# An attention block followed by eight experts: the first expert's loads put into the last batch, powers two experts ahead, gate rows apart, last output through six PSUM banks

## The chip, the cores and the metric

The kernel runs on one core of one Trainium2 chip. The metric is device time in microseconds of one execution; the time before is the median of three runs. The profile is of one further execution. Engines are called as the profile calls them: PE (TensorE, matmuls; PEld is its weight load), DVE (VectorE), ACT (ScalarE), POOL (GpSimd) and SP (SyncE, which here only issues transfers).

## What is computed

The block takes x of 16 batches x 1024 rows x 256 columns, all in float32. From a condition vector per batch come six modulation vectors (shift, scale and gate for each of two halves; a gate keeps its sign and a size of at least 0.25).

- First half: h = layernorm(x) * (1 + scale) + shift. Then an attention layer on h: another layernorm with gamma and beta, q, k and v projections with biases, rotary positions, 16 heads of 16 columns, causal softmax, output projection, and h added again. x = x + gate * that.
- Second half: h = layernorm(x) * (1 + scale) + shift with the second set of vectors, read as one list of 16384 rows. Eight experts each take 512 rows of h (their row numbers are given; a row may be drawn by several experts and more than once by one), compute gelu(rows W1 + b1) W2 + b2 (256 to 1024 to 256 columns), times a combine weight, and add the result to the rows. Only the first 2048 of the combine weights' rows exist; larger row numbers take the last one. x = x + gate * the sum.

## The kernel before, in words

The kernel has a start, an attention stage and an experts stage. On PE, DVE, ACT and POOL the order of the instructions is the order of the program, written out by hand (`manual_schedule`). SP is not in that list: its transfers are placed by the framework's scheduler, by when they become ready in its own model, and the queue is then fixed. So a transfer that waits holds those behind it in SP's queue.

**Start.** The modulation vectors are computed (lines 112 to 143) and written to two tables in device memory, `mod_a` for the first half and `mod_b` for the second, 3 x 256 columns each. Weights and rotary tables are loaded and turned (165 to 216). Two buffers in device memory, `ops`, in which the operands of the score products are laid out per head as 32 rows, get their fixed rows filled by 64 small transfers (line 259). Then the first batch's x is loaded and prepared.

**Attention.** Batches are worked one after another. A batch has four groups of four heads, a group twelve blocks: `(c, j)`, c the half of the 1024 queries (512 each), j the block of 128 keys, causal ones only. Per block and head, `product` in `attend` (line 513) makes the scores in a tile of the PSUM pool `ps_s` (six banks, tag `s`), ACT makes the exponential (526), POOL masks the diagonal blocks (528), and `values` (549) multiplies with v one block later. In the same block the *next* group's row maxima are found (`maxima`: PE 455, DVE 467 and 471), in banks of the same pool. `place` sends them through device memory into the operands (491, 492). All other work of a batch hangs in the list `extra`, at a block number: preparation of the next batch, the layernorms of the one after, and the output projection of the batch before (`project`: `turn` at 591 transposes, ACT copies at 592, `out_` at 598 multiplies with Wo, DVE 608 multiplies with the gate, POOL 611 adds x for two row blocks at once, and SP 612 writes them to `out`). `wide` and `narrow` are lists of block numbers in a batch; `t` and `w` are these for the batch at hand. The projection's `pn` and `pw` tiles are in pool `ps_1`, tag `misc`, with one bank. x of a batch stays in SBUF from its load to its output; four buffers (`bufs=4`, line 269) rotate.

The last batch has no next batch, so its last group has no maxima beside it. Its own output projection has nothing to hide behind: half 0 is turned at the last two blocks, and the rest follows after the last block:

```
        behind[0](*blocks[-1])
        behind[1](1)()
        for items in [proj[B - 1][0][1], *proj[B - 1][1]]:
            for item in items:
                item()
```

**Experts.** Their pools (`fc`, `fw`, `fk`, `fps`) open when the attention's have closed, in the same memory. Each expert e has these steps:

- `weights(e)`: SP loads W1, W2 and b2, two buffers each.
- `rows_mod(e)`: POOL gathers, per 128 rows, the second half's modulation rows (768 columns, four gathers). `rows_x(e)`: four gathers of x's rows from `out`. A gather is one POOL instruction (line 102).
- `hidden(e)`: statistics on DVE (818, 821), the power -0.5 on POOL (823, 824), normalizing on DVE (827), scale and shift (830, 831).
- `turned(e)`: eight transposes on PE (840), DVE copies (841). `first(e)`: 32 matmuls (849), ACT's gelu (852), which starts with a table load.
- `often(e)`: how often each row occurs in the expert's list, on DVE (859 to 861), from `tokb`, a copy of all lists in every partition (four transfers of 512 KB, line 892).
- `rows_now(e)`: four gathers of the rows of `out` as they are now (`cur`).
- `second(e)`: 64 matmuls (874) in four products of 128 rows; DVE adds b2 (877), multiplies with count, weight and gate (878), adds `cur` (881); POOL scatters the 128 rows to `out` (883). PSUM holds two such products.

All rows of x for all experts must have been gathered before the first scatter. The order of the stage is the end of the program: `weights(0)`, `weights(1)`, `rows_mod(0)`, `rows_x(0)`, `often(0)`, `hidden(0)`, `turned(0)`, `rows_mod(1)`, `rows_x(1)` to `rows_x(7)`, and then for each expert `hidden(e + 1)`, `first(e)`, `often(e + 1)`, `turned(e + 1)`, `rows_now(e)`, `second(e)`, `weights(e + 2)`, `rows_mod(e + 2)`.

Of the kernel before, what the change touches and what calls it, by code (L numbers as in the profile page):

```python
# [19 lines left out]
P = 128  # L20
# [7 lines left out]
def adaln_block_kernel(  # L28
# [81 lines left out]
    mod_b = dram.tile([B, 3 * D], F32, name="mod_b")  # L110


    with tc.tile_pool(name="mod", bufs=1) as mp, tc.tile_pool(
# [17 lines left out]
        for half, dst in ((0, mod_a), (1, mod_b)):  # L131
# [11 lines left out]
            nc.sync.dma_start(out=dst[:, :], in_=m3)  # L143
# [14 lines left out]
    )  # L158
    with ExitStack() as actx:
# [107 lines left out]
        def load(b):  # L267
            s = S[b]
            s["x"] = two.tile([P, NT, D], F32, name=f"x_{b}", tag="x", bufs=4)
# [311 lines left out]
        def project(b):  # L581
# [4 lines left out]
            def turn(c, k):  # L586
                if k == 0:
                    oTs[c] = wk.tile([P, KC, QC], F32, name=f"onT_{b}_{c}", tag="onT")
                pt = ps_1.tile([P, TC, P], F32, name=f"pn_{b}_{c}_{k}", tag="misc")
# [4 lines left out]
            def out_(c, t):  # L594
                t0 = c * TC + t
                po = ps_1.tile([P, D], F32, name=f"pw_{b}_{t0}", tag="misc")
# [12 lines left out]
                if t % 2 == 0:  # L609
                    return  # L610
# [77 lines left out]
        for b in range(B):  # L688
# [19 lines left out]
            if b > 0:  # L708
# [8 lines left out]
            if b + 1 == B:  # L717
                pn, pw = proj[b][0]
                each(pn, [at0 + NG * NS - 2, at0 + NG * NS - 1])
# [12 lines left out]
        for b in range(B):  # L732
            for G in range(NG):
# [3 lines left out]
                for n, (c, j) in enumerate(blocks):  # L737
# [29 lines left out]
                    if n == NS - 2 or n == 2 and behind:  # L767
                        turn()
# [5 lines left out]
        for items in [proj[B - 1][0][1], *proj[B - 1][1]]:  # L774
            for item in items:
                item()


    FF = W1.shape[2]
    NF = FF // P  # L780

# [6 lines left out]
    X = [dict() for _ in range(E)]  # L788
# [3 lines left out]
    times = fc.tile([P, E, NCT], F32, name="times")  # L792

    def weights(e):
        s = X[e]
        s["w1"] = fw.tile([P, KC, FF], F32, name=f"w1_{e}", tag="w1")
        nc.sync.dma_start(out=s["w1"], in_=W1[e].rearrange("(k p) f -> p k f", p=P))
        s["w2"] = fw.tile([P, NF, D], F32, name=f"w2_{e}", tag="w2")
        nc.sync.dma_start(out=s["w2"], in_=W2[e].rearrange("(k p) d -> p k d", p=P))
        s["b2"] = fw.tile([P, D], F32, name=f"b2_{e}", tag="b2")  # L800
        nc.sync.dma_start(out=s["b2"], in_=b2[e].partition_broadcast(P))

    def rows_mod(e):
        X[e]["mod"] = fw.tile([P, NCT, 3 * D], F32, name=f"modg_{e}", tag="modg")
        for t in range(NCT):
            gather(X[e]["mod"][:, t, :], mod_b[:, :], bidx[:, t, e : e + 1])

# [3 lines left out]

    def hidden(e):

        s = X[e]
        xe = xg[:, e, :, :]
        st = fk.tile([P, NCT, 6], F32, name=f"fst_{e}", tag="fst")
        for t in range(NCT):
            nc.vector.bn_stats(st[:, t, :], xe[:, t, :])
        mv = fk.tile([P, NCT, 2], F32, name=f"fmv_{e}", tag="fmv")
        for t in range(NCT):  # L820
            nc.vector.bn_aggr(mv[:, t, :], st[:, t, :])
        rstd = fk.tile([P, NCT], F32, name=f"frstd_{e}", tag="frstd")
        nc.gpsimd.tensor_tensor(rstd, mv[:, :, 1], eps[:, :NCT], ALU.add)
        nc.gpsimd.tensor_tensor(rstd, rstd, mhalf[:, :NCT], ALU.pow)
        hn = fk.tile([P, NCT, D], F32, name=f"hn_{e}", tag="hn")
        for t in range(NCT):
            nc.vector.tensor_scalar(
                hn[:, t, :], xe[:, t, :], mv[:, t, 0:1], rstd[:, t : t + 1], ALU.subtract, ALU.mult
            )
# [38 lines left out]
    def second(e):  # L868
        s = X[e]
        y = fk.tile([P, NCT, D], F32, name=f"fy_{e}", tag="fy")  # L870
        for t in range(NCT):
            po = fps.tile([P, D], F32, name=f"fo_{e}_{t}", tag="fo")
            for f in range(NF):
# [5 lines left out]
                y[:, t, :], y[:, t, :], times[:, e, t : t + 1], s["mod"][:, t, 2 * D : 3 * D], ALU.mult, ALU.mult  # L879
# [16 lines left out]
    weights(0)  # L896
    weights(1)
    rows_mod(0)
    rows_x(0)
    often(0)  # L900
    hidden(0)
    turned(0)
    rows_mod(1)

    for e in range(1, E):
        rows_x(e)
    for e in range(E):
# [3 lines left out]
        if e + 1 < E:  # L911
            often(e + 1)
            turned(e + 1)
        rows_now(e)
        second(e)
# [72 lines left out]
```

## Time and profile before

| what | value |
|---|---|
| time, median of 3 runs | 3397.24 us (3396.8 to 3398.42) |
| time of the profiled execution | 3397.8 us |
| its span, first to last instruction | 3396.1 us |
| mean granted clock of PE | 0.953 |
| busy: PE, DVE, ACT, POOL | 3138.8, 2308.1, 1727.4, 1216.3 us |
| last matmul of values in the attention (line 549) starts | 3065.77 us |
| last output rows issued (line 612) | 3089.72 us |
| first matmul of the first expert (line 849) | 3116.99 us |
| first matmul of the second expert (line 849) | 3174.99 us |

The page cuts the span into 40 equal slices of 85 us. A digit is the busy share of an engine in that slice, in tenths; the row PEclk is the clock that PE was granted, in tenths of full speed:

```profile
PE   1589999999999999999999999999999999994888
DVE  1267777877777777777777777777777777652544
ACT  0135656565555565555555565656565655551111
POOL 1334243333434343334343434333342443114443
PEclk6579999999999999999999999999999999997899
DMA  6101011121111111111111111212111111004442
```

The attention fills slices 3 to 36, the experts the last four.

### The profile page before, as it was taken

Reading aid. Unit: us, or ns where it says so; the run is one execution under the profiler, and the core shown is the slowest. Engines: PE = TensorE matmul, PEld = TensorE weight load, DVE = VectorE, ACT = ScalarE, POOL = GpSimd, SP = SyncE. Lnnn points to the kernel's source line nnn. Section 1 sums busy time; section 2 is a strip of 40 time slices with the busy share of each in tenths; the row PEclk is TensorE's granted clock in tenths of the full one; section 3 lists DMA queues with packets and bytes.
Section 4 is the critical chain, followed back from the end, with each engine's and each line's share of the span. In section 5 each row is a group of like instructions: output and inputs, shape, how many; then the busy total and the mean of one; then the engine's idle time right before and its main releaser. Section 6 shows DMA issues by size and latency. Waiting matters only on the chain.

```text
span 3396.1 us, 62141 instructions
## 1 busy us (share of the span) xinstructions
PE 3138.8 (92%) x22497; PEld 1371.5 (40%) x22497; DVE 2308.1 (68%) x6919; ACT 1727.4 (51%) x3916; POOL 1216.3 (36%) x1338
## 2 busy tenths in 40 slices
PE   1589999999999999999999999999999999994888
PEld 0244344434344444444444444344434444332556
DVE  1267777877777777777777777777777777652544
ACT  0135656565555565555555565656565655551111
POOL 1334243333434343334343434333342443114443
PEclk6579999999999999999999999999999999997899
DMA  6101011121111111111111111212111111004442
GB/s 149 48 19 51 27 45 62 39 68 38 57 45 46 55 48 58 46 56 48 47 51 50 54 53 42 65 39 68 33 62 40 49 43 46 33 11 165 148 148 88
DMA packets 105827, 199.10 MB, mean 59 GB/s; under 512 B 14704, under 2 KB 60176, under 8 KB 105520
## 3 DMA queue, kind: packets, MB, share of 16 engines
q1 hardware_dynamic: 97328, 169.83, 16.2%
q0 software_dynamic: 8192, 25.31, 2.3%
q8 instruction: 177, 2.90, 0.4%
q14 instruction: 130, 1.06, 0.1%
HBM read 135.21 MB, written 59.88 MB: 57 GB/s over the span
## 4 chain that ended last, share of the span: by engine, by line
PE 80%; POOL 4%; ACT 4%; DVE 3%; issue 3%; DMA 1%; POOLq 0%; DVEq 0%; ACTq 0%
PE s L513 35%; PE o L549 17%; PE pqk L370 8%; PE m L455 5%; PE pv L397 4%; PE pw L598 4%; PE fo L874 3%; ACT p L526 3%; POOL p L528 2%; PE pn L591 1%; PE ptx L354 1%; ACT h L307 1%; DMA modg<-mod_b,bidx 1%; DVE mt L467 1%; PE pm L487 1%
## 5 line engine op out<-in xcount | busy, mean ns | idle before, releaser
L526 ACT ACTIVATE p<-s 128x512 f32<-128x512 f32 (+3 forms) x3072 | 1336.1, 489 | 1066.5 <-PE m L455 970.1
L455 PE MATMUL m<-ko,qo 32*128 32x512 f32 (+3 forms) x6144 | 1590.0, 541 | 10.4 <-DVE mt L471 7.0
L513 PE MATMUL s<-qo,ko 32*128 32x512 f32 (+3 forms) x6144 | 1486.3, 537 | 2.7 <-ACT p L526 0.4
L467 DVE TENSOR_REDUCE mt<-m 128x1 f32<-128x512 f32 x1024 | 658.3, 685 | 233.0 <-PE m L455 204.7
L513 PEld LDWEIGHTS s<-qo,ko 32*128 32x128 f32 x6144 | 513.2, 184 | 666.2 <-issue 474.1
L528 POOL TENSOR_SCALAR_AFFINE_SELECT p<-p 128x512 f32<-128x512 f32 x512 | 325.9, 637 | 1055.6 <-ACT p L526 1054.6
L471 DVE CUSTOM_DVE_ANT_0 masked<-m,dmask,mt 128x512 f32<-128x512 f32 (+3 forms) x1024 | 562.3, 549 | 203.8 <-PE m L455 101.1
L549 PE MATMUL o<-p,v_pad 128*32 128x512 f32 (+3 forms) x6144 | 656.0, 499 | 47.4 <-POOL p L528 44.5
L471 DVE CUSTOM_DVE_ANT_0 masked<-m,dmask 128x512 f32<-128x512 f32 (+3 forms) x1024 | 501.2, 489 | 265.8 <-PE m L455 177.3
L455 PEld LDWEIGHTS m<-ko,qo 32*128 32x128 f32 x6144 | 574.5, 185 | 64.0 <-DVE mt L471 25.5
L370 PE MATMUL pqk<-xnT,wqk 128*128 128x256 f32 x1024 | 307.8, 425 | 15.4 <-DVE rot L376 13.7
L549 PEld LDWEIGHTS o<-p,v_pad 128*32 128x32 f32 x6144 | 121.2, 108 | 487.9 <-POOL p L528 260.6
L370 PEld LDWEIGHTS pqk<-xnT,wqk 128*128 128x128 f32 x1024 | 183.6, 200 | 215.3 <-issue 119.9
L389 POOL TENSOR_TENSOR rot<-rot,rot 128x512 f32<-128x512 f32 x64 | 81.6, 1275 | 374.1 <-DVE rot L376 290.3
L611 POOL TENSOR_TENSOR y<-y,x 128x512 f32<-128x512 f32 x64 | 81.8, 1279 | 303.2 <-DVE y L608 265.2
L471 DVE DVE_READ_ACCUMULATOR2_ANT mt<- 128x1 f32 x2048 | 169.7, 83 | 0.2
L320 POOL TENSOR_TENSOR h<-h,mod 128x512 f32<-128x512 f32 x128 | 162.6, 1274 | 5.6 <-ACT h L307 4.2
L376 DVE SCALAR_TENSOR_TENSOR rot<-pqk,bcol,cosT 128x256 f32<-128x256 f32 x256 | 122.9, 480 | 57.1 <-PE pqk L370 46.4
L598 PE MATMUL pw<-wo_sb,onT 128*128 128x256 f32 x512 | 148.5, 413 | 4.9 <-DVE y L608 3.3
L852 ACT ACTIVATE gT<-ph,b_sb 128x512 f32<-128x512 f32 x64 | 43.9, 687 | 209.9 <-PE ph L849 190.6
L397 PE MATMUL pv<-wv_sb,xnT 128*128 128x256 f32 x512 | 147.4, 411 | 3.3 <-ACT v_pad L404 2.3
L598 PEld LDWEIGHTS pw<-wo_sb,onT 128*128 128x128 f32 x512 | 88.7, 193 | 106.5 <-issue 47.5
(105 smaller groups left out, 2346.7 us busy)
## 6 DMA issues: line engine op xcount, KB each, us to landing
ops<-rot SPq DMA_DIRECT2D x128, 256.0 KB
qo<-ops SPq DMA_DIRECT2D x64, 512.0 KB
ko<-ops SPq DMA_DIRECT2D x64, 512.0 KB
x<-in_x_dram SPq DMA_DIRECT2D x16, 1024.0 KB
out_dram<-y SPq DMA_DIRECT2D x64, 256.0 KB
w<-in_W_dram SPq DMA_DIRECT2D x16, 1024.0 KB
mod<-mod_a SPq DMA_DIRECT2D x16, 384.0 KB
ops<-zeros SPq DMA_DIRECT2D x62, 64.0 KB
```

The source lines that it names most:

```text
L320: nc.gpsimd.tensor_tensor(h, h, row(n), op)
L370: nc.tensor.matmul(ps, lhsT=wqk[:, k, n, e, :], rhs=xt[:, k, ts(u, QW)], start=(k == 0), stop=(k == KC - 1))
L376: nc.vector.scalar_tensor_tensor(s["rot", e, f][:, ts(u, QW)], ps, bcol[:, n, e : e + 1], tab[:, half * QC + u * QW : half * QC + (u + 1) ...
L397: nc.tensor.matmul(pv, lhsT=S[b]["xnT", t // TC][:, k, ts(t % TC, P)], rhs=wv_sb[:, k, :], start=(k == 0), stop=(k == KC - 1),)
L455: nc.tensor.matmul(sc[:, 0:w], lhsT=q[rows, ts(i, P)], rhs=k[rows, c * QC : c * QC + w], start=True, stop=True,)
L467: nc.vector.tensor_reduce(dst, sc[:, 0:w], AX.X, ALU.max, negate=True)
L471: nc.vector.tensor_tensor_reduce(out=masked[:, 0:w], in0=sc[:, 0:w], in1=dmask[:, QC - w : QC], scale=-1.0, scalar=mt[half][:, 0, h, i % T ...
L513: nc.tensor.matmul(sc[:, 0:w], lhsT=k[rows, ts(j, P)], rhs=q[rows, q0 : q0 + w], start=True, stop=True,)
L526: nc.scalar.activation(p[:, h, 0:w], sc[:, 0:w], AF.Exp, scale=scale)
L528: nc.gpsimd.affine_select(out=p[:, :, 0:P], in_=p[:, :, 0:P], compare_op=ALU.is_ge, fill=0.0, base=0, pattern=[[0, GH], [1, P]], channel_m ...
L549: nc.tensor.matmul(acc[c][W * g : W * (g + 1), QC - w : QC], lhsT=v[:, j, h * VW : h * VW + W], rhs=ps[c, j][:, g, 0:w], start=(j == 0), s ...
L598: nc.tensor.matmul(po, lhsT=oTs[c][:, k, ts(t, P)], rhs=wo_sb[:, k, :], start=(k == 0), stop=(k == KC - 1),)
```

## The change

In the text of the program:

- A pool `big` with four buffers of 8 KB per partition is opened before the attention's pools and stays to the end. x of the batches, W1 and W2 of all experts and the first expert's modulation rows take its buffers in turn. W1, the modulation rows and W2 of the first expert are placed in the last batch: W1 and the tile at block 2, the four gathers at blocks 4 to 7 of group 1, W2 at block 8 of group 2.
- `mod_b` loses the gate columns; they get a table `mod_g` and gathers of their own (`rows_gate`).
- In the last batch the projection of the batch before moves to earlier blocks. Half 0 of the last batch's own projection is done within its last group (turned at blocks 7 and 8, multiplied at 8 to 11), after `turn` of half 0 at block 6 instead of 10. The tiles `pn` and `pw` of the last batch are taken from the six banks of `ps_s`. For half 1 DVE adds x and each 128 rows are written by themselves.
- In the experts `hidden` is split: `stats(e)` on DVE, `powers(e)` on POOL, and the rest. Statistics and powers of expert e + 2 and its modulation rows come within expert e, ahead of `second(e)`. Before the loop the gathers of x for experts 1 and 2 come first, then the second expert's powers, then the first expert's gate rows, then the x rows of experts 3 to 7. `often(0)` stays ahead of the first statistics.

The diff, cut to its core:

```
     mod_a = dram.tile([B, 3 * D], F32, name="mod_a")
-    mod_b = dram.tile([B, 3 * D], F32, name="mod_b")
+    mod_b = dram.tile([B, 2 * D], F32, name="mod_b")
+    mod_g = dram.tile([B, D], F32, name="mod_g")
...
-            nc.sync.dma_start(out=dst[:, :], in_=m3)
+            if half == 0:
+                nc.sync.dma_start(out=mod_a[:, :], in_=m3)
+            else:
+                nc.sync.dma_start(out=mod_b[:, :], in_=m3[:, 0 : 2 * D])
+                nc.sync.dma_start(out=mod_g[:, :], in_=g)
...
+    big = ctx.enter_context(tc.tile_pool(name="big", bufs=4))
...
+    def big_tile(shape, name):
+        return big.tile(shape, F32, name=name, tag="x")
+
+    def weights_1(e):
+        X[e]["w1"] = big_tile([P, KC, FF], f"w1_{e}")
+        nc.sync.dma_start(out=X[e]["w1"], in_=W1[e].rearrange("(k p) f -> p k f", p=P))
+
+    def weights_2(e):
+        X[e]["w2"] = big_tile([P, NF, D], f"w2_{e}")
+        nc.sync.dma_start(out=X[e]["w2"], in_=W2[e].rearrange("(k p) d -> p k d", p=P))
+
+    def first_mod():
+        X[0]["mod"] = big_tile([P, NCT, 2 * D], "modg_0")
+
+    def rows_mod(e, t):
+        gather(X[e]["mod"][:, t, :], mod_b[:, :], bidx[:, t, e : e + 1])
...
-            s["x"] = two.tile([P, NT, D], F32, name=f"x_{b}", tag="x", bufs=4)
+            s["x"] = big_tile([P, NT, D], f"x_{b}")
...
-                pt = ps_1.tile([P, TC, P], F32, name=f"pn_{b}_{c}_{k}", tag="misc")
+                if b + 1 == B:
+                    pt = ps_s.tile([P, QC], F32, name=f"pn_{b}_{c}_{k}", tag="s").rearrange("p (t q) -> p t q", q=P)
+                else:
+                    pt = ps_1.tile([P, TC, P], F32, name=f"pn_{b}_{c}_{k}", tag="misc")
...
-                po = ps_1.tile([P, D], F32, name=f"pw_{b}_{t0}", tag="misc")
+                if b + 1 == B:
+                    po = ps_s.tile([P, QC], F32, name=f"pw_{b}_{t0}", tag="s")[:, :D]
+                else:
+                    po = ps_1.tile([P, D], F32, name=f"pw_{b}_{t0}", tag="misc")
...
-                if t % 2 == 0:
+                if (b, c) == (B - 1, NC - 1):
+                    nc.vector.tensor_tensor(y[:, t % 2, :], y[:, t % 2, :], s["x"][:, t0, :], ALU.add)
+                    nc.sync.dma_start(
+                        out=out[b * L + t0 * P : b * L + (t0 + 1) * P, :], in_=y[:, t % 2, :]
+                    )
+                if t % 2 == 0 or (b, c) == (B - 1, NC - 1):
                     return
...
-            if b > 0:
+            if b + 1 == B:
+                for c, (pn, pw) in enumerate(proj[b - 1]):
+                    each(pn, t[2 * c : 2 * c + 2])
+                    each(pw, w[8 * c + 8 : 8 * c + 12])
+                at(2, [lambda: weights_1(0), first_mod])
+                at(2 * NS + 8, [lambda: weights_2(0)])
+                for n in range(NCT):
+                    at(NS + TC + n, [lambda n=n: rows_mod(0, n)])
+                end = at0 + 3 * NS + mid + 3
+                pn, pw = proj[b][0]
+                each(pn, [end, end + 1])
+                each(pw, range(end + 1, end + 5))
+            elif b > 0:
                 for c, (pn, pw) in enumerate(proj[b - 1]):
                     each(pn, t[3 + 2 * c : 5 + 2 * c])
                     each(pw, (w[18:22], w[26:30])[c])
...
-            if b + 1 == B:
-                pn, pw = proj[b][0]
-                each(pn, [at0 + NG * NS - 2, at0 + NG * NS - 1])
...
-                    if n == NS - 2 or n == 2 and behind:
+                    if n == (NS - 2 if units else mid + 2) or n == 2 and behind:
                         turn()
...
-        for items in [proj[B - 1][0][1], *proj[B - 1][1]]:
+        for items in proj[B - 1][1]:
...
+    def stats(e):
         st = fk.tile([P, NCT, 6], F32, name=f"fst_{e}", tag="fst")
         for t in range(NCT):
-            nc.vector.bn_stats(st[:, t, :], xe[:, t, :])
+            nc.vector.bn_stats(st[:, t, :], xg[:, e, t, :])
         for t in range(NCT):
-            nc.vector.bn_aggr(mv[:, t, :], st[:, t, :])
+            nc.vector.bn_aggr(mv[:, e, t, :], st[:, t, :])
+
+    def powers(e):
+        nc.gpsimd.tensor_tensor(rstd[:, e, :], mv[:, e, :, 1], eps[:, :NCT], ALU.add)
+        nc.gpsimd.tensor_tensor(rstd[:, e, :], rstd[:, e, :], mhalf[:, :NCT], ALU.pow)
...
-    weights(0)
-    weights(1)
-    rows_mod(0)
+    bias_2(0)
...
     rows_x(0)
     often(0)
+    stats(0)
+    powers(0)
     hidden(0)
     turned(0)
-    rows_mod(1)
-
-    for e in range(1, E):
+    later_mod(1)
+    rows_x(1)
+    rows_x(2)
+    stats(1)
+    powers(1)
+    rows_gate(0)
+
+    for e in range(3, E):
         rows_x(e)
+    weights_1(1)
+    weights_2(1)
+    bias_2(1)
     for e in range(E):
         if e + 1 < E:
             hidden(e + 1)
...
             often(e + 1)
             turned(e + 1)
+        if e + 2 < E:
+            stats(e + 2)
         rows_now(e)
+        if e + 1 < E:
+            rows_gate(e + 1)
+        if e + 2 < E:
+            powers(e + 2)
+            later_mod(e + 2)
         second(e)
         if e + 2 < E:
-            weights(e + 2)
-            rows_mod(e + 2)
+            weights_1(e + 2)
+            weights_2(e + 2)
+            bias_2(e + 2)
```

`later_mod(e)` is four `rows_mod(e, t)` into a tile of its own pool, `rows_gate(e)` four gathers from `mod_g`.

## The prediction

> **What bounds the kernel now.** I read the page's 40 slices first: TensorE is at 90% or more from the fourth slice to the 36th, then falls to 4 and 8, its clock row falls to 7, and the DMA row, at 0 to 2 since the second slice, rises to 4. So the attention is bound by TensorE, and what can be won lies in the last 350 us. I then read the chain of waits between attention and experts.
>
> ```profile
> 3068.54 1.11 PE pw L598 x4
> ...
> 3077.87 2.09 PE pw L598 x4
> ...
> 3084.46 3.96 issue
> 3088.46 1.24 POOL y L611
> 3089.72 3.34 DMA out_dram<-y
> 3093.12 0.72 issue
> 3093.84 0.96 POOL modg L102
> ...
> 3102.70 6.12 DMA xg<-out_dram,idx
> ...
> 3124.47 28.93 issue
> 3153.40 0.07 DVE hn L827
> ```
>
> The columns are start, length, what. Eight output projections go one by one through a single PSUM bank, then the last rows are written, then four gathers of modulation rows stand ahead of the four of x. The 28.93 us are no idle engine. The timeline of GpSimd shows what runs in them:
>
> ```profile
> 3123.55 0.94 POOL L102 DMA_INDIRECT xg<-out_dram,idx  x1 [0.30 <-issue]
> ...
> 3151.06 0.95 POOL L102 DMA_INDIRECT xg<-out_dram,idx  x1 [0.30 <-issue]
> 3152.03 0.21 POOL L823 TENSOR_TENSOR frstd<-fmv,eps 128x4 f32<-128x4 f32 x1
> 3152.32 1.05 POOL L824 TENSOR_TENSOR frstd<-frstd,mhalf 128x4 f32<-128x4 f32 x1
> ```
>
> The second expert's power is queued behind 28 gathers, one per 1.255 us. TensorE waits 24.85 us for it (its transposes at 3157.47). In the experts stage, the same timeline:
>
> ```profile
> 3254.83 1.00 POOL L883 DMA_INDIRECT out_dram<-fy,idx  x1 [6.62 <-DVE fy L881]
> 3260.96 0.99 POOL L883 DMA_INDIRECT out_dram<-fy,idx  x1 [5.12 <-DVE fy L881]
> 3264.18 0.97 POOL L883 DMA_INDIRECT out_dram<-fy,idx  x1 [2.23 <-DVE fst L818]
> 3270.59 0.97 POOL L883 DMA_INDIRECT out_dram<-fy,idx  x1 [5.44 <-issue]
> ```
>
> Each scatter writes `out` and waits until the one before has landed: 3.2 us is the usual spacing (2.41 to land and 0.77, as the chain's last scatter shows), 6.1 and 6.4 are two slow landings. Behind them stood the modulation rows and the power that the next expert needed, so this expert took 39.1 us (chain: fo at 3248.59, then 3287.72), the others 29.1 to 30.8.
>
> **Start of the kernel.** x moves into a pool that opens ahead of the attention's weights, so those should no longer share memory with the modulation stage and can load before 20.8 us, when they waited for mod_b. The first x is issued by SP at 68.23, behind 64 fill transfers of about 0.64 us, 54 of them after tok_d at 33.38. SP idles 7.7 us ahead of tok_d, which waits for work that waited for mod_b (2 us less now). Some fills change places with the weights' loads; the extra write for the gate rows takes SP 0.4 us. I take -1.2, ends -6 and +4.
>
> **Last batch.** Eight pw and four pn of batch 14 move about 12 blocks earlier, out of the last group. In groups whose blocks also compute maxima a pw costs little: four values steps with pw beside them (3008.73 to 3025.52) took 16.8 us, four without (2966.21 to 2982.38) 16.2, so 0.15 to 0.2 each. Four more pw and one more pn there: +1.1. In the last group blocks 4 to 7 lose their pw and go from TensorE's 3.13 us (s 1.07, o 1.0, pw 1.06) to about 2.3; blocks 7 to 11 take over two pn and four pw, and there pw waits for ACT's copies, which stand behind four exponentials. Placing these by hand gives -0.6. Together +0.5, ends -3 and +4 (the s banks, now shared by scores and projections, are the doubt: a wait for one exponential, 0.5 us, at some of 18 places). The last values end at 3066.7 instead of 3066.2. Four gathers of modulation rows (5 us of GpSimd) and 2 MB of weights fall into these groups of the last batch, in the view by windows:
>
> ```profile
> 2915.50:2957.20 41.70, 39.66 (x302) 15.74 (x298) 28.31 (x85) 23.18 (x54) 5.09 (x9) 1.00 0.08 27
> 2957.20:2999.00 41.80, 39.69 (x306) 15.91 (x309) 28.25 (x85) 22.96 (x54) 5.09 (x9) 1.00 0.01 2
> ```
>
> The columns are window, length, busy time of PE, PEld, DVE, ACT and POOL, granted clock, DMA share, GB/s. With GpSimd 12% busy and DMA at 1 to 8% they cost nothing; without that cover 5 us. SP now also issues w1 and w2 there, 0.4 us each and each after the rows of x whose buffer it takes; ahead of a row of maxima in SP's queue such a wait would hold the next group, so I bound it at 3 us and take nothing, since x loads of 1 MB and operand loads pass the same queue in every earlier batch.
>
> **Tail of the attention.** From the values' end to o ready stays 2.2 us: 3068.9. Then two pn, two copies, about 2.1: 3071.0. Then only four pw, back to back, 1.14 each: 3075.5. Two DVE steps of 0.43 replace DVE plus GpSimd's 1.24 and what GpSimd waited: 3076.5. With 3.34 landing and 0.72 the first gather of x starts at 3080.5 instead of 3098.87. The clock is a choice. [...] In this trace no gap before 3078 exceeds 0.9 us, and yet the clock row goes 1.00, 0.98, 0.50 and pw from 1.11 to 2.09. By the row they might cost 3.8 more. I take warm, because the drop came 12 us after the values ended and these pw end 9 us after them; 3.8 goes into the range.
>
> **First power.** `often(0)` now stands ahead of the statistics on DVE and needs tokb, whose transfers wait for the last pw. Before, 11.0 us passed from the first issue (3088.28) to DVE's start (3099.29), with weights and modulation gathers beside it; 10.4 now, since only one weight load (1 MB) competes: 3086.4. `often` 4.8, statistics 1.7, power with its gaps 1.4: 3094.2, against 3110.95. x lands earlier (last gather at 3084.3, landing 2.45 to 6.1). Saved 16.7, ends 12 and 20. The weights themselves were all but hidden: the first transposes (3115.12) began 0.2 us after hn was ready, though the view of waits names a small transfer queued behind the weights as what came last.
>
> **A new wait.** After the power come 12 gathers (15.1), the second expert's powers (1.5), 4 gate gathers and 20 of x for experts 3 to 7 (30.1): only then `cur` of the first expert, at +46.7, landing 2.45 later. hn of the second expert is in time (+20.6, transposes at +21.7, as the first products took 21.7 before). But `second(0)` has written three of its four products by +33 and two banks are held: DVE stands in the addition of cur until +49.2. The fourth product starts at +50.1, cold (16 matmuls, about 5.5): the second expert's ph starts at +55.7. Before, it was 3174.99 - 3110.95 = 64.0. So 8.3 are saved of the 24.85 that the power cost; the rest moves into the wait for cur. In absolute terms 3149.9.
>
> **Experts.** TensorE alone: seven times 13.73 + 13.83, six transposes of 1.07, 7.9 after the last product: 207.3; before it took 221.1. Powers and modulation rows now have an expert's time to spare. But GpSimd's round is cur 5.3, gate 5.0, powers 1.5, mod 5.0, scatters 3 x 3.2 + 2.7 = 29.1, against TensorE's 28.6, in order, and the scatters now stand behind the mod gathers, which stand behind powers, which wait for DVE's `stats(e + 2)` after `turned`. With cur late from the start there is little slack: about +2.4. If the two slow landings come again they cost 2.9 and 3.2; I count half, 3: 212.7, saved 8.4, ends 2 and 13. [...] The timeline has gathers of 1.15, 1.37 and 1.88 us beside DVE's work where 0.95 is usual, about 0.6 per round, already in my 5.3. I take the row.
>
> **Sum.** 1.2 + 16.7 + 8.3 + 8.4 = 34.6 off the span of 3396.1: 3361.5. The profiled run took 3397.8, 1.7 around its span; the median of 3397.24 is 0.56 below that. So 3362.6, say 3363.
>
> **Rivals.**
> - The seam comes late: tokb's transfers go ahead of the last output rows, or TensorE is cold in the tail, or tokb gains nothing from the weights' absence: +4 to +10, 3371. For it: the cold row and the 6.12 us landing. Chance 0.15.
> - No wait for cur: if its rows came before `second(0)` adds them, ph would start at +36.6, 19 us earlier: 3344. Against it: the steady 1.255 us per gather and the order of the diff. Chance 0.06.
> - Slower: GpSimd's round becomes the bound. With four scatters in series behind the gathers, each excess over 3.2 counts four times per expert. At the slow 6.3 it is 12.4 per expert, some 75 in all: 3438. It decides from 34.6 / 24 = 1.4 us excess, a spacing of 4.6. Against it: three slow ones (6.1, 6.4, 5.2) among some 24. Chance 0.06, and 0.03 for about that point itself, no change.
> - My forecast: 0.70.
>
> **How the numbers follow.** The measurement tells about 0.2%, 6.8 us, from no change. The first two rivals and the forecast are faster: 0.91; same 0.03; slower 0.06. The ends of the parts won't all fall on one side; with about two thirds of them together 44 are saved at best and 22 at worst, 3353 to 3375. The range reaches from there to 3379 for the late seam and to 3348 towards the case without the wait.
>
> **What would show it.** Right: the x gathers start near 3080 with no modulation gathers ahead; the first power ends near 3094; TensorE idles about 17 us inside the first expert's fo, while DVE waits for cur; ph to ph 28.7 to 29.4. Wrong: TensorE runs through `second(0)`; fo waits in later experts for hn; the first x load leaves 68 us by more than 6; groups of the last batch grow past 43 us.

## The result, and the profile after

| | before | after |
|---|---|---|
| median of 19 runs each | 3396.97 us (3386.57 to 3399.21) | 3377.99 us (3367.7 to 3392.28) |
| ratio | | 0.9954, 95% interval 0.994 to 0.9968 |
| profiled execution: time, span, clock of PE | 3397.8, 3396.1, 0.953 | 3390.29, 3388.6, 0.951 |

The change saves 0.46%, some 16 us (19 by the two medians); forecast were 34, 1.0%. The runs of after lie 25 us apart, and their times follow the clock that PE was granted (3368 at 0.959, 3391 at 0.951). The profiled one is among the long ones, so I compare it stage by stage.

The end of the attention came about as worked out. PE's timeline has the four last projections in one piece, warm (14 of their 16 matmuls in 3.29 us; before, each of the last four projections, of 4 matmuls, took 2.07 to 2.09 us). GpSimd's has no modulation gather ahead of x:

```profile
3077.55 3.29 PE L632 MATMUL pw<-wo_sb,onT 128*128 128x256 f32 x14 [0.24 <-ACT onT L623]
```

```profile
3084.35 0.96 POOL L102 DMA_INDIRECT xg<-out_dram,idx  x1 [9.04 <-DMA out_dram<-y]
...
3098.28 1.05 POOL L862 TENSOR_TENSOR frstd<-frstd,mhalf 128x4 f32<-128x4 f32 x1
...
3115.70 1.05 POOL L862 TENSOR_TENSOR frstd<-frstd,mhalf 128x4 f32<-128x4 f32 x1
```

From the end of the last values (3073.97) to the first gather of x pass 10.4 us (before 32.7), to the end of the first power 25.4 (before 44.75). The second power is 17.4 us behind the first, before it was 42.4. The forecast wait is there too, on DVE and then on PE:

```profile
3151.37 0.43 DVE L923 TENSOR_TENSOR fy<-fy,cur 128x256 f32<-128x256 f32 x1 [22.28 <-DMA cur<-out_dram,idx]
```

```profile
3152.19 5.36 PE L916 MATMUL fo<-w,gT 128*128 128x256 f32 x16 [19.68 <-DVE fy L923]
3157.39 3.60 PE L891 MATMUL ph<-hT,w 128*128 128x512 f32 x8
```

But from the first power to the end, where 16.7 us should have been saved, after takes 289.3 us and before 285.1. GpSimd's timeline shows why one has to look there. This is one expert's round, between two groups of scatters:

```profile
3178.99 0.97 POOL L925 DMA_INDIRECT out_dram<-fy,idx  x1 [2.20 <-DVE times L902]
3181.66 0.99 POOL L102 DMA_INDIRECT cur<-out_dram,idx  x1 [1.70 <-DMA out_dram<-fy,idx]
...
3186.74 0.95 POOL L102 DMA_INDIRECT gate<-mod_g,bidx  x1 [0.30 <-issue]
...
3191.77 1.04 POOL L862 TENSOR_TENSOR frstd<-frstd,mhalf 128x4 f32<-128x4 f32 x1
3193.01 1.02 POOL L102 DMA_INDIRECT modg<-mod_b,bidx  x1 [0.19 <-issue]
...
3198.17 1.00 POOL L925 DMA_INDIRECT out_dram<-fy,idx  x1 [0.30 <-DVE fy L923]
```

From the landing of a scatter on GpSimd never waits in it: twelve gathers and two instructions of the power fill 16.5 us, and the next scatter goes 0.30 us behind the last gather. So I split the stage at the first scatter: from the first power it comes after 55.6 us before, after 65.9 us with the change, since cur, gate and modulation rows stand ahead of it. From there to the end it is 229.6 and 223.3.

### The profile page after: what moved, and what is told of

It reads as the page before. It is cut to its first block, busy times and chain, and to the rows that moved or that the text cites. A ratio compares the mean times of both kernels' runs of the same rounds, so it can differ in the third digit from the quotient of the medians.

```text
span 3388.6 us, 62205 instructions
## 1 busy us (share of the span) xinstructions
PE 3144.8 (93%) x22497; PEld 1370.1 (40%) x22497; DVE 2307.9 (68%) x6923; ACT 1727.9 (51%) x3916; POOL 1243.9 (37%) x1368
## 5 line engine op out<-in xcount | busy, mean ns | idle before, releaser
L483 PEld LDWEIGHTS m<-ko,qo 32*128 32x128 f32 x6144 | 576.3, 186 | 63.2 <-DVE mt L499 25.5
L916 PE MATMUL fo<-w,gT 128*128 128x256 f32 x512 | 114.8, 384 | 22.2 <-DVE fy L923 19.7
```

What stands on the lines that cost most here:

```text
L483: nc.tensor.matmul(sc[:, 0:w], lhsT=q[rows, ts(i, P)], rhs=k[rows, c * QC : c * QC + w], start=True, stop=True,)
L916: nc.tensor.matmul(po, lhsT=s["gT"][:, f, ts(t, P)], rhs=s["w2"][:, f, :], start=(f == 0), stop=(f == NF - 1))
```

## The experiments

All ratios are to runs of the kernel before on the same chip; a kernel has 4 to 22 runs. The last four columns are from the profiled execution: from the end of the first power to the first scatter, from there to the end, their sum, and the distance from one expert's ph to the next from the third expert on.

| kernel | median, us | ratio, 95% interval | power to scatter | scatter to end | sum | ph to ph |
|---|---|---|---|---|---|---|
| before | 3396.97 | 1 | 55.6 | 229.6 | 285.1 | 28.8 to 40.1 |
| after | 3377.99 | 0.9954 (0.994 to 0.9968) | 65.9 | 223.3 | 289.3 | 28.4 to 31.2 |
| e1 | 3367.31 | 0.9905 (0.9885 to 0.9925) | 60.9 | 220.8 | 281.7 | 29.8 to 34.3 |
| e2 | 3383.57 | 0.9947 (0.9931 to 0.9963) | 57.0 | 242.1 | 299.1 | 28.4 to 36.1 |
| e3 | 3378.81 | 0.9923 (0.9907 to 0.9939) | 51.8 | 239.2 | 291.0 | 31.1 to 33.9 |
| e4 | 3375.5 | 0.9929 (0.9908 to 0.995) | 66.0 | 218.8 | 284.9 | 29.6 to 31.2 |
| e5 | 3382.81 | 0.9957 (0.9941 to 0.9973) | 57.0 | 240.3 | 297.2 | 28.9 to 36.1 |
| e6 | 3365.85 | 0.992 (0.9898 to 0.9943) | 65.8 | 217.1 | 282.8 | 28.4 to 29.4 |
| e7 | 3366.46 | 0.9912 (0.9895 to 0.9929) | 65.8 | 227.5 | 293.3 | 28.4 to 33.1 |
| e8 | 3387.63 | 0.9975 (0.9966 to 0.9985) | 84.2 | 219.4 | 303.6 | 29.3 to 35.3 |
| e9 | 3380.57 | 0.9969 (0.9956 to 0.9981) | 55.6 | 229.5 | 285.1 | 29.2 to 39.1 |
| e10 | 3362.44 | 0.9907 (0.9893 to 0.9921) | 60.5 | 227.2 | 287.7 | 28.4 to 35.3 |
| e11 | 3365.2 | 0.9917 (0.9904 to 0.993) | 60.7 | 225.5 | 286.2 | 28.4 to 36.5 |
| e12 | 3359.95 | 0.9897 (0.9881 to 0.9913) | 60.6 | 229.9 | 290.5 | 28.4 to 36.9 |
| e13 | 3347.39 | 0.9856 (0.9841 to 0.9871) | 61.2 | 210.9 | 272.2 | 28.4 |
| e14 | 3341.18 | 0.9839 (0.9826 to 0.9853) | 55.7 | 209.4 | 265.2 | 28.4 |
| e15 | 3336.93 | 0.9827 (0.9813 to 0.984) | 56.2 | 209.4 | 265.6 | 28.4 |

**e1, no gathers for the first cur.**

```
     def rows_now(e):
+        if e == 0:
+            X[e]["cur"] = xg[:, 0, :, :]
+            return
```

> The changed kernel, except that the first expert adds its products to the rows of x that it gathered already (no scatter has come between, so they are the same rows): the four gathers of cur(0) are gone, and DVE has nothing to wait for in second(0). My theory: TensorE's 19.7 us of standing inside the first expert's fo go, and the second ph starts near first power + 37 instead of + 58. But GpSimd is still in the 20 gathers of x until first power + 42, then does 4 gate rows, powers, 4 modulation rows and four scatters in series, so cur of the second expert comes near + 76, and TensorE stands in the second expert's fo instead: of the 20 us about 10 to 14 stay, median near 3366 against 3378. The 11.5 us in which all of TensorE, ScalarE and VectorE stood after 3157.4 in the changed kernel: if they come from the gathers in flight, they show again at an earlier place; if they come of the wait for cur itself, they go, and the median falls nearer 3355. Rival (the loss lies in the attention's clock, not here): the time moves by less than 5 us.

TensorE's stop is gone and the second ph starts at first power + 37.1, 21 us earlier than in after. The first scatter comes only 5.0 us earlier, which is the issue of four gathers. The ratio improved more than that; e10 against e7 below, where the clock doesn't blur it, gives 4 us by the medians and 2 by the ratios. So of TensorE's 20 us nearly all was given back. In e1's profile one sees where: in the next expert its transposes waited 15.17 us for hn, whose power stands behind the x gathers.

**e2 and e3, gate and modulation rows between the scatters**, e3 with e1's edit.

```
     rows_now(e)
-        rows_gate(e + 1), powers(e + 2), later_mod(e + 2)
+        powers(e + 2)
     second(e), after each scatter t:
+        gate row t of e + 1, modulation row t of e + 2
```

> The changed kernel, except that GpSimd issues each gate row of the next expert and each modulation row of the one after it behind a scatter, instead of all eight ahead of the four scatters: they then fill the 2.4 us in which a scatter lands and the next one waits. GpSimd's round falls from about 29 + slow landings to about 5.3 (cur) + 1.5 (powers) + 4 x 3.5 = 21. My theory (GpSimd's round sets the experts' pace): the distance from one expert's ph to the next becomes 28.0 to 28.7 everywhere instead of 28.4 to 31.2, the waits of hn for modg and of fo for DVE behind cur vanish, and the last 190 us shorten by 8 to 11: median near 3368. Rival (the pace is set by TensorE and by something that stalls it, not by GpSimd): no change within 3 us. Rival (gathers between the scatters lie in the same queue and delay their landing): spacing of the scatters grows over 4.5 us and the time stays or grows. The wait for cur(0) and the stall after it stay as they were.

> Both edits: no gathers for the first expert's cur, and gate and modulation rows between the scatters. My theory: GpSimd comes to the first scatter at first power + 43, to cur of the second expert near + 62 and of the third in time, so the third ph starts near first power + 72 (changed kernel: + 99.8) and the rest runs at TensorE's 28.6 per expert: about 30 to 38 us less than the changed kernel, median 3340 to 3350, 11 of it open, since the stall that followed the wait may come again elsewhere. Rival (the stall belongs to the gathers in flight): 3350 to 3356. Rival (the loss is the attention's clock): both edits together give under 10 us.

Both expectations missed: the stretch from scatter to end grew to 242 and 239. GpSimd's queue was shorter, but two waits came in: its powers for the statistics, and DVE's hn for the modulation rows that now came last.

```profile
3211.70 0.19 POOL L871 TENSOR_TENSOR frstd<-fmv,eps 128x4 f32<-128x4 f32 x1 [6.72 <-DVE fmv L868]
```

```profile
3233.95 1.23 DVE L882 TENSOR_TENSOR hn<-hn,modg 128x1024 f32<-128x1024 f32 x1 [11.86 <-DMA modg<-mod_b,bidx]
```

Both lines are e2's. DVE stands in hn with the statistics behind it, GpSimd stands for the statistics with the scatters behind it: a ring through two queues that are kept in order. So e2 doesn't tell whether the number of gathers matters.

**e4 and e7, a filler for the clock.** In after, PE's clock fell to half eleven times in the attention, once a batch at most; before, seven times (two of them short). The view by windows of after, around one drop (window, length, busy PE, PEld, DVE, ACT, POOL, granted clock, DMA share, GB/s):

```profile
612.61:616.03 3.42, 3.42 (x37) 1.75 (x36) 2.98 (x15) 1.32 (x4) 1.93 (x4) 1.00 0.00 0
616.03:619.44 3.41, 3.29 (x26) 1.99 (x26) 2.35 (x13) 2.33 (x7) 0.15 (x1) 1.00 0.13 28
619.44:622.86 3.42, 3.42 (x21) 1.31 (x22) 1.40 (x4) 2.79 (x8) 1.87 (x2) 0.50 0.74 284
622.86:626.27 3.41, 3.41 (x12) 1.29 (x8) 1.40 (x4) 1.29 (x4) 0.55 (x1) 0.50 0.02 5
```

The drop follows a stretch in which PE was busy 3.29 of 3.41 us. A batch with such a drop takes 180.8 to 181.4 us, one without 178.1 to 178.7. On the guess that more work on PE would hold the clock, e4 and e7 add two products whose result nobody reads, at two different boundaries between groups:

```
+        def filler():
+            pf = ps_s.tile([P, QC], F32, name="pf", tag="s")
+            nc.tensor.matmul(pf[:, :D], lhsT=ident, rhs=wo_sb[:, 0, :], start=True, stop=True)
...
e4: blocks 10 and 11 of group 3; e7: blocks 10 and 11 of group 0
```

> The changed kernel, with two matmuls that are not needed (128x256 by a full 128x128 array, result unread) put into the last two blocks of every batch but the last, where TensorE otherwise has only score products on 32 rows and 128 columns. Theory: the drops of the granted clock to half for 6.8 us at batch boundaries (11 in the profiled run of the changed kernel, 7 in that of the kernel before) [...] with the filler they all vanish, the mean clock of every run is 0.962 or more, the runs lie within 5 us of each other instead of 25, and the time is 14 x (1.1 minus some idle) = 8 to 14 above the best case of 3360, so 3366 to 3374. Rival (the drops are no matter of this place): they stay, the spread stays 20 us or more, and the median rises by 8 to 14 to about 3388.

> The filler of the run e4 at another place: the drops of the clock lie not at the batch boundary, as I wrote there, but at the boundary from the first to the second group of heads of a batch[...]. Two unneeded 128x256 matmuls now go into the last two blocks of the first group of every batch. Theory: the drops go, mean clock 0.961 or more in every run, runs within 6 us of each other (25 now), median 3360 + 15 x 0.5 = 3366 to 3370. Rival [...]: drops stay at any boundary, the spread stays near 20, the median rises to 3384.

At e4's place, which I had taken for that of the drops, the runs stay 21 us apart (3366.01 to 3387.05, clock 0.954 to 0.961). At e7's they lie within 4 us (3366.31 to 3370.14, every clock 0.961), and the profile has one short drop. So the drops belong to the boundary from group 0 to group 1 (in every profile all of them stand at the end of group 0), and they make the spread of after.

**e5, the gate joined again, behind the scatters.**

```
-    mod rows (512 columns) and gate rows (256) of e + 2 and e + 1, ahead of second(e)
+    one row of 768 columns of e + 2, behind second(e)
```

> The changed kernel with one part of the change undone: from the second expert on, the gate is gathered in one row with the two other modulation rows (768 values, four gathers per expert instead of eight), behind the scatters, as before the change; powers stay two experts ahead, the first expert's early rows and weights stay. My theory (GpSimd's round was made the bound by the four gathers that the separate gate adds): the round falls from 29.1 to about 24, GpSimd catches up after the first expert, the scatters follow fo at once and so leave the stretch in which the next 1 MB weight load passes; ph to ph becomes 28.6 to 29 from the third expert on (now 28.4 to 31.2), scatter spacings are 3.2 to 3.5 with few exceptions, and first power to end falls from 285 to 289 to about 270: median 3362 to 3368. Rival (the bound is the chain scatter, landing, cur, addition, scatter, not the number of gathers): ph to ph stays at 30, no gain over 3 us.

The rival's number came, but not for its reason. The modulation rows, late again as in e2, hold DVE and with it PE:

```profile
3242.60 1.94 PE L884 MATMUL fpt<-ident,hn 128*128 128x128 f32 x8 [5.32 <-DVE hn L875]
```

Two things had been changed at once, the number and the place. e13 separates them.

**e6, no weight loads from the fourth expert on** (experts 4 to 8 compute with weights and biases of the expert two before, in place of their own).

```
-            weights_1(e + 2), weights_2(e + 2), bias_2(e + 2)
+            for w in ("w1", "w2", "b2"): X[e + 2][w] = X[e][w]     # e > 0
```

> The changed kernel without the weight and bias loads of experts 3 to 7 (they use those of the expert two before; that part of the computation is changed). Theory: a scatter takes 5.3 to 7.7 us instead of 3.2 when a 1 MB weight load passes beside it, and in the changed kernel these loads, which start when fo frees their buffer, meet the scatters that GpSimd's late round issues behind fo. Then from the second expert's scatters on every spacing is 3.2 to 3.7 and ph to ph falls by 1 to 1.5 us to about 29.1, GpSimd's round without slow landings: 5 to 7 us less in all. Rival (slow landings come of the gathers' own queue): spacings above 5 stay, one per expert, and the time stays within 2 us.

The mean spacing of scatters in the first five rounds is 3.74 us, against 4.31 in after (4.56 in e7), ph to ph 28.4 to 29.4, scatter to end 6.2 less than in after. Two spacings of 4.9 and 5.8 stay; the first is beside the one such load that e6 still makes, the second beside none. The profile of e4, which has all the loads, comes near (mean spacing 3.92, 218.8 to the end), so a single profile says little. The runs say more: at a clock of 0.957 to 0.958 those of e6 took 3364 to 3366 us, those of after 3371 to 3374. What passes beside a slow landing shows in the windows of after, each from one scatter to the next:

```profile
3165.25:3168.89 3.64, 0.00 (x0) 0.00 (x0) 0.00 (x0) 0.00 (x0) 1.01 (x2) 0.57 0.36 122
3168.89:3175.82 6.93, 3.76 (x5) 1.70 (x6) 6.51 (x12) 1.27 (x2) 0.98 (x2) 0.50 0.55 189
3175.82:3178.99 3.17, 3.17 (x9) 1.44 (x8) 3.03 (x7) 1.38 (x2) 0.97 (x2) 0.97 0.12 41
3198.17:3201.85 3.68, 3.68 (x13) 2.12 (x12) 1.59 (x5) 0.69 (x1) 1.00 (x1) 1.00 0.49 150
3201.85:3207.20 5.35, 5.35 (x13) 2.30 (x13) 5.21 (x10) 2.06 (x3) 0.99 (x2) 1.00 0.68 234
3207.20:3210.40 3.20, 3.20 (x9) 1.47 (x8) 2.82 (x6) 1.37 (x2) 1.00 (x2) 1.00 0.11 41
```

3.2 us go with 41 GB/s, 5.35 and 6.93 with 234 and 189: 1.25 to 1.3 MB, a weight load, the scatter itself and little else. It starts when the last fo frees w2's buffer. Before, the last scatter followed that fo at once, and the load fell behind it:

```profile
3199.69:3202.89 3.20, 3.20 (x17) 2.81 (x16) 1.33 (x3) 0.00 (x0) 0.98 (x1) 1.00 0.11 41
3202.89:3206.12 3.23, 3.23 (x12) 1.91 (x11) 1.98 (x6) 0.27 (x1) 0.97 (x2) 1.00 0.36 68
3206.12:3214.00 7.88, 7.88 (x20) 3.51 (x19) 1.38 (x9) 3.16 (x5) 6.36 (x8) 1.00 0.98 332
```

**e8, cur added one expert later**, so that its rows have a round to come.

```
     second(e): fy without cur, no scatter
+    third expert: statistics, powers and modulation rows ahead of the last x rows
+    next expert, behind turned: add cur (first expert: x rows), scatter, gate and modulation row between
```

> The changed kernel with cur's addition and the scatters of an expert put one expert later (behind the transposes of the expert after next, where the gathered rows have had a whole round to come), the first expert using its x rows, gate and modulation rows between scatters, modulation and power of the third expert gathered ahead of the last x rows. Theory (TensorE waits only for GpSimd's chain scatter, landing, cur, addition): with a round of slack TensorE never stands in fo; second ph at first power + 37, ph to ph 27.6 to 28.7 throughout, first power to end 37 + 7 x 28.3 + 30 = 265 or less, against 282 to 289: median 3350 to 3358. Rival (DVE or the weight loads take the place of the wait): ph to ph above 29.5, time like e1's 3367.

A miss: the second ph started early (first power + 37.2), but the first scatter came at + 84.2, and the time rose. It follows the scatter, not the ph. But e8 isn't clean. DVE's addition is behind the transposes of a later expert there, and GpSimd stood 21.54 us for statistics in the same queue; PE came to these transposes only at 3160.66, since it had stood 26.05 us in the ph before them, which is the matter left open below.

**e9, the filler in the kernel before; e10, e1 and e7 together.**

> The kernel before, with the filler of e7 (two unneeded matmuls in the last blocks of the first group of every batch) and nothing else. It shows what the change does when neither kernel's clock drops in the attention. The profiled run of before had five long and two short drops (2.8 and about 1.1 us each): 3397 - 16 + 8.5 for the filler = 3389, with runs within 4 us. Against e7's 3366.5 the change is then worth 22 to 23 us. Rival (the drops hid a larger gain: before had fewer of them than the changed kernel): before with the filler stays near 3397 or above and the change is worth 30 or more.

> The changed kernel with the edits of e1 (the first expert adds to the rows of x that it has) and of e7 (filler). If both gains are of separate causes they add: e7's 3366.5 less the 8 to 12 us by which e1's stretch from first power to end (281.7) is shorter than e7's (293.3): 3355 to 3358, with all runs within 6 us. Rival (e1's gain was fewer drops of the clock): 3364 or more.

Without drops the change is worth 0.9912 / 0.9969 = 0.994, about 19 us (14 by the medians, which are from two chips; 22 to 23 were expected). That is no more than the interval of the plain comparison holds, so the clock makes the spread but doesn't hide a larger gain. Three of e9's nine runs show 0.957 or 0.958 and are 7 to 11 us longer, so the filler doesn't end the drops in every run there. e10 stands 4 us below e7 (2 by the ratios), between what the theory and its rival had forecast, and its first scatter comes 5.3 earlier after the first power.

**e11, w2 loaded later, by ScalarE; e12, also the first x ahead of the fills.**

```
             gelu of block f
+            if f == NF // 2 and 0 < e < E - 1:
+                w2 and b2 of e + 1, issued by nc.scalar
```

> e10 with the loads of w2 and b2 of the expert after next issued by ScalarE in the middle of the next expert's ph, instead of by SyncE when the last fo frees the buffer: about 7 us later, when that expert's four scatters should have landed. Theory (slow landings come of this 1 MB load, as e6 showed by leaving loads out): scatter spacings fall to 3.2 to 3.7 except where w1 still meets one, ph to ph falls by 1 to 2 us per expert, 5 to 8 us below e10. Rival (the load meets cur's gathers instead, which TensorE waits for as well): no gain, or up to 5 us worse.

> e11 with the first x loaded ahead of the 64 fill transfers instead of behind them (it left at 63 us). Theory: the statistics, norms and first products of batch 0 start up to 37 us earlier, and only the rows that pass through the operand buffer wait for the fills: 15 to 30 us below e11. Rival (the fills themselves, or the products' weights, are what the first scores wait for): within 3 us of e11.

In e11 the scatters of three experts are 3.2 to 3.7 us apart and PE runs at 28.4 per expert. Then PE stops, as it has run ahead of GpSimd:

```profile
3267.72 10.53 PE L932 MATMUL fo<-w,gT 128*128 128x256 f32 x48
3283.26 6.54 PE L932 MATMUL fo<-w,gT 128*128 128x256 f32 x16 [5.01 <-DVE fy L935]
```

Scatter to end is 225.5, no better than e10's 227.2, since the load now met the landing of a group's last scatter (from there to the next group 19.8 us, then 23.5 and 21.1), and further on the scatters again (spacings of 4.8 to 7.0). The rival was right. A faster PE gains nothing here: GpSimd sets the end. e12's values ended 4.4 us earlier than e11's, not 15 to 30.

**e13 to e15, the gate joined in its place.** Three buffers let the joined row stay ahead of the scatters, so that in GpSimd's queue nothing changes but the number of gathers; with the filler. e14 adds e1's edit, e15 also e11's and e12's.

```
-        X[e]["mod"] = fw.tile([P, NCT, 2 * D], F32, name=f"modg_{e}", tag="modg")
+        X[e]["mod"] = fw.tile([P, NCT, 3 * D], F32, name=f"modg_{e}", tag="modg", bufs=3)
...
+        X[e]["gate"] = X[e]["mod"][:, :, 2 * D : 3 * D]
...
-        if e + 1 < E:
-            rows_gate(e + 1)
```

> e7 (changed kernel with filler) with the gate gathered in one row with the modulation from the second expert on, in the same place of GpSimd's queue (three buffers make that possible): four gathers fewer per expert, and nothing else moved. Theory (GpSimd's queue is the bound): first power to first scatter 60.9 (e7: 65.8); scatter round 24 to 26 where TensorE allows it, so TensorE's 28.4 sets the pace and ph to ph is 28.0 to 28.8; first power to end 265, or 275 if TensorE's late completion comes and now costs, against e7's 293.3: median 3338 to 3348. Rival (the chain scatter, landing, cur, addition sets the pace, or the weight loads beside the scatters): first power to end above 287, median 3360 to 3367.

> e13 with the first expert's cur taken from its x rows (e1). Theory: first scatter at first power + 55.9, cur of the second expert at + 76, its last fo near + 80 and the third ph near + 82 instead of + 87: 5 to 6 us below e13, 3333 to 3342. If TensorE's late completion costs here, up to 10 more. Rival (e1's gain was only the four gathers' issue, hidden once the queue has room): same as e13 within 2 us.

> e14 with w2 and b2 issued by ScalarE in the middle of ph (e11) and the first x ahead of the fills (e12). Theory: x 4 us (as e12's last values came 4.4 earlier than e11's), and slow landings no longer delay cur: 0 to 4 us more, so 4 to 8 below e14. Rival: with GpSimd not the bound the landings don't matter, 4 only.

All three medians fell into their ranges. One round of GpSimd in e13, DVE's first addition of that round's cur, and PE beside it:

```profile
3206.90 0.99 POOL L102 DMA_INDIRECT cur<-out_dram,idx  x1 [2.24 <-DMA out_dram<-fy,idx]
...
3215.03 1.02 POOL L102 DMA_INDIRECT modg<-mod_c,bidx  x1 [0.19 <-issue]
...
3220.11 1.00 POOL L933 DMA_INDIRECT out_dram<-fy,idx  x1 [0.30 <-DVE fy L931]
3224.81 1.92 POOL L933 DMA_INDIRECT out_dram<-fy,idx  x1 [3.70 <-DVE hn L877]
3231.62 0.97 POOL L933 DMA_INDIRECT out_dram<-fy,idx  x1 [4.89 <-DVE times L910]
```

```profile
3212.53 0.45 DVE L931 TENSOR_TENSOR fy<-fy,cur 128x256 f32<-128x256 f32 x1
```

```profile
3193.29 13.90 PE L899 MATMUL ph<-hT,w 128*128 128x512 f32 x32
3207.02 1.04 PE L890 MATMUL fpt<-ident,hn 128*128 128x128 f32 x8
3207.90 13.98 PE L924 MATMUL fo<-w,gT 128*128 128x256 f32 x64
3221.71 13.90 PE L899 MATMUL ph<-hT,w 128*128 128x512 f32 x32
```

PE runs without a gap, 28.42 us from ph to ph. The slow landings are still there (4.7 and 6.8 us here, mean 4.76, more than in after). They take up what the four gathers left: GpSimd's first five rounds last 29.2 us on average, and it waits in them for little but landings. That is now close enough to TensorE's pace: the first rows of cur are issued 5.6 us before DVE adds them, and TensorE doesn't stand for them in these rounds. Against e7, with four gathers per expert as the only difference (and the third buffer that they need), the first scatter comes 4.6 us earlier and the rest takes 16.6 less; the median fell by 19. e15 is some 59 us, 1.7%, below the kernel before.

## Why the prediction was half right

**Start and last batch: better than forecast, both small.** The first x left at 63.25 instead of 68.23, 5.0 earlier; of this 2.2 were left at the first groups (forecast 1.2). The last batch, from its first to its last values, took 1.8 less where I had +0.5.

**Tail: right.** Values to first x gather 10.4 us (forecast 13.8). I had taken these pw as warm, and they were (14 of their 16 matmuls in 3.29 us at a granted clock of 1.00). They ended 6.9 us after the values; in before the clock fell 11.7 after them, in after 9.9. In the 3.41 us ahead of the fall PE had 1.6 us of work in before and 0.4 in after, so what lets the clock fall the two runs don't show.

**First power: right.** 25.4 us after the values (forecast 27.5); of the gain against before, 19.4 came where 17.2 stood in the sum (44.75 to 27.5).

**A new wait: there, at its place and length, and not what matters.** DVE resumed at first power + 52.0 (forecast 49.2), the second ph began at + 58.1 (forecast 55.7, before 64.0). But I stopped the count at cur. Behind cur GpSimd had still to issue four gate rows, two powers and four modulation rows before the first scatter. By my own figures that is 46.7 + 5.0 + 5.0 + 1.5 + 5.0 = 63.2; measured were 65.9, against 55.6 before. e10 took the wait away and gained 2 to 4 us of 20, no more than the issue of its four gathers.

**Experts: the step that failed.** It says "TensorE alone: ... 207.3", adds "about +2.4" for GpSimd and, for slow landings, "I count half, 3". From first power to end this gave 55.7 + 212.7 = 268.4; after took 289.3, e4 and e7 with the same experts' part 284.9 and 293.3. The round of 29.1 that I had worked out for GpSimd was right (the measured rounds, less the excess named below, take 29.0), and had to be summed instead of TensorE's: 63.2 to the first scatter, five rounds of 29.1, and the last three experts as measured, 61.6, make 270.3. So the place of the sum was wrong by little and one term by much: the five rounds took 161.7, not 145.5. The excess of their fifteen scatter spacings over 3.2 us adds up to 16.7, where 3 stood; 14.2 of it are in six spacings beside 0.7 MB or more of a weight load. Of the two slow landings of before that I had counted by half, one was of this kind and the other had nothing but itself to move (23 GB/s):

```profile
3254.83:3260.96 6.13, 6.13 (x31) 5.38 (x30) 2.67 (x6) 0.00 (x0) 1.01 (x2) 1.00 0.07 23
3264.18:3270.59 6.41, 6.41 (x16) 2.85 (x15) 1.26 (x8) 2.75 (x4) 0.97 (x2) 1.00 0.59 197
```

The first kind came once in before. A GpSimd that comes late after fo meets the load in nearly every expert. What makes a landing slow without a load (6.1 and 5.2 in before, 5.8 in e6) stays open. e6, without the later loads, has an excess of 8.1 (e4 and e7, with them, 10.8 and 20.4). e13 shows that the slow landings cost this much only together with the four gathers of the separate gate: without these the round, slow landings and all, is nearly TensorE's.

**The sum of the parts.** Start 2.2, last batch 1.8 and first power 19.4 less, experts 4.1 more: 19.3 us saved, as e7 against e9 gives by the ratios. The profiled pair differs by 7.5 only; four more drops of the clock took the other 12. Against the forecast start and last batch were 3.3 better and the first power 2.2, and the experts 20.8 worse. The 5.5 us that the small parts gave beyond their forecasts are luck.

**The rivals.** The slower one, with chance 0.06, had this mechanism and priced it: decisive from an excess of 1.4 us in a spacing. The mean excess was 1.1, which ate most of the gain and not all. "No wait for cur" would have given 19 us more by my sum; e10 shows that it doesn't.

**What stays open.** In after, DVE and SP got the end of the first expert's last fo 11.6 us late:

```profile
3169.14 0.42 DVE L919 TENSOR_TENSOR fy<-fo,b 128x256 f32<-128x256 f32 x1 [14.71 <-remote]
```

PE's record of these matmuls ends at 3157.5, and two ph that it shows right after them reached ACT only at 3171.32. The like is in before (ACT idle 6.34 us), in e6 to e15 (PE stands 3.4 us in e13, 19 to 20 in e14 and e15, 25 to 26 in e8 and e10 to e12), always between the first and the second expert, while gathers are in the queue, and not in e1 to e5. I found neither an instruction fetch nor a transfer that ends with it, and made no experiment on it. While GpSimd sets the end it is mostly hidden, as far as I can tell; in e14 the third ph came 5 us later than expected, and it may be the cause.

## What to carry to other kernels

Find the queue that sets the end after the change, and sum along that one: where another engine's queue is full, a wait that is shortened on TensorE is worth only what that queue gets back (here 2 to 4 us of 20). A gather that is split in two costs its issue twice (1.25 us each here), in every round, and an engine that is a little late may come under a transfer that it used to miss (scatters of 5.3 to 7.7 us beside a weight load here, where 3.2 is usual). Split the time at an event of that queue (here the first scatter), and compare the two parts over all variants before believing a chain of waits.

## What the runs showed of the hardware that I had not expected

- PE's clock fell to half with PE 96% busy in the 3.41 us before (ten of the eleven drops of after; 86% in the other), by a profile that models the ends of matmuls. Most of the products there use 32 of 128 rows. The drops stand on a grid: one of the eleven lasts 3.413 us, ten last 6.827, twice that, and all stretches at half clock in a profile, before's too, start whole multiples of 3.413 us apart. Nine drops in a row in after are 180.91 us apart, 53 times 3.413. A batch with a drop lasts as long (180.8 to 181.4 us), so the next batch meets the grid at the same phase, which I take for the reason why it drops again. Two full-array products of 0.6 to 0.7 us at that place ended it in the profiled runs (e7, e9 to e15: none or one). A 1 MB operand load begins at the same boundary (the 284 GB/s above), but in e7 too. Whether these products or waits that this busy time hides are what counts was not tried apart.
- A scatter of 128 rows takes 3.2 us to let the next one go, and 5.3 to 7.7 beside a whole 1 MB load on another queue in after (4.6 to 6.3 in e4 and e6).
